# Keys kept unnormalised in the first layer of a four-layer network: their inverse norms reach the taps' sums through memory

## The chip, the cores and the metric

One core of a Trainium2 chip runs the whole network in one launch. The metric is the device time in microseconds (us). Three runs of the kernel before took 5038.33, 5038.93 and 5039.8 us; the median is 5038.93.

## What is computed

Four layers run one after the other over two images of 512 channels and 64 x 64 pixels, all in float32. Only the first layer matters here. It is an attention with 8 heads of 64 channels, in which each pixel attends to the 3 x 3 window around itself (nine "taps") and to 256 pooled tokens:

```python
q_norm = _l2norm(q)                                  # per pixel and head
q_scaled = (q_norm + query_embedding[None]) * softplus(temperature)[None]
k_l = _l2norm(k_l.reshape(B, N, nh, hd)).reshape(B, N, C)
...   # k_local, v_local: the 3 x 3 patches of keys and values, zeros outside the image
attn_local = jnp.einsum('bhnd,bhndk->bhnk', q_scaled, k_local)
attn_pool = jnp.einsum('bhnd,bhpd->bhnp', q_scaled, _l2norm(k_pool))
attn = softmax(concatenate([attn_local, attn_pool], -1), -1)
lt = jnp.einsum('bhnd,hdk->bhnk', q_norm, learnable_tokens) + learnable_bias[None] + a_local
x_local = jnp.einsum('bhnk,bhndk->bhnd', lt, v_local)
```

A score of a tap is a sum over the 64 channels of a head of query times key. The key's norm is one number for each pixel and head, so it may be multiplied into the key before the sum or into the sum after it.

## The kernel before

**Tiling.** Channels lie on the 128 partitions, so a tile holds two heads; there are four such chunks (`cc`). Pixels run along the free dimension. A unit is 1024 pixels (16 image rows) of one chunk: four units a chunk, 16 units an image, each in two halves `j` of 512 pixels. Keys and values of a chunk lie in SBUF as padded images `kx` and `vx` of 66 x 66 with zeros in the frame, so that a tap is a shifted view of them.

**Steps.** `Local.run` (L2046) is a software pipeline: in step `i` (from -4 to 16) several generators advance in turn, one round of all of them after the other, some ten rounds a step. In step `i`

- `projections` (L2349) projects keys of unit `i+4` and queries of unit `i+3` on TensorE (four matmuls of 128x512 for each half, by the helper at L134), and values. ScalarE reads each bank twice: once with the bias into `kraw` or `qn` (L2359), once squared into `sq` (L2361).
- `norms` (L2385) sums the squares that the step before left (L2395), and VectorE turns them (L2398), takes inverse roots by three Newton steps (L2401 to L2408) and turns them back into rows (L2410).
- `normed` (L2414) spreads a row over the 64 partitions of its head by a matmul with two rows of weights (L2422), and VectorE multiplies the raw keys into `kx` and the queries into `qn` (L2430): keys in one round, queries in the next. `learned` (L2438) then makes the learned tokens' term (L2445, L2448) and the scaled queries (L2450).
- `tap_products` (L2462) multiplies the scaled queries of unit `i+1` with the nine shifted views of `kx`, two taps in one instruction (L2473). The third of these is held until the last multiply of `normed` has been issued. `tap_sums` (L2490) sums the products over the channels of a head into one bank `tap` (L2500): row `32q + 2k + h` is tap `k` and head `h`, where `q` is 2 times the half plus `k % 2`. ScalarE takes Exp of that bank (L2508).
- `attend` (L2512) does unit `i`: scores against pooled tokens (L2525), Exp (L2529), values (L2535), sums (L2551, L2554), division, and stores the taps' weights to memory, `rows` (L2592).
- `weigh` (L2612) does unit `i-1`: ten weights (number 0 for the pooled part, 1 to 9 for taps) are fetched from memory, spread over 64 partitions each (L2610, two transfers a weight), copied to PSUM by ScalarE (L2626), multiplied by VectorE (L2634, L2631) and added by GpSimd (L2639). Three buffers take turns, so a fetch waits for the addition three weights before.

Before step 1 the pooled tokens are made (`pooled_tokens`, L2093) and their keys and values (`pooled_heads`, L2133), whose matmuls stand at L2151, L2160, L2177, L2211 and L2217. After the last unit the layer's output is projected.

**What sets the order.** PSUM gives five banks `mm` in a ring to everything but the queries' copy `qs` and the bank `tap`. From step 1 to step 11 (`steady`) TensorE keeps the order in which the program is written; the other engines, and all of them in the other steps, are put in order by a scheduler at build time. All transfers are issued by SyncE (SP), in order.

Of the kernel before, what the change touches and what calls it, by code (L numbers as in the profile page):

```python
# [9 lines left out]
F32 = mybir.dt.float32  # L10
I32 = mybir.dt.int32
AF = mybir.ActivationFunctionType
# [4 lines left out]
P = 128  # L17
# [1950 lines left out]
class Local:  # L1968
# [9 lines left out]
    def __init__(self, net, X, Y, sp_scale, d, wp, yp, pp, ppt, pps):  # L1978
# [3 lines left out]
        nc, new = self.nc, lambda shape, name: wp.tile(shape, F32, name=name)  # L1982

        self.yd = yp.tile([P, KC, N], F32, name="yd")
        self.wd = yp.tile([3, P, KC, C], F32, name="wd")
        self.rows = cycle([yp.tile([P // 2, self.UT], F32, name=f"rows{i}") for i in range(2)]).__next__

# [37 lines left out]
        self.raw = {"k": self.kraw, "q": self.qn}  # L2025
# [20 lines left out]
    def run(self):  # L2046


        self.nmean = self.net.stats[:, 0]
        xs = self.pooled_tokens()  # L2050
        heads = self.pooled_heads(xs)
        units = KC * self.UN
        unit = lambda u: u if 0 <= u < units else None
        self.pending = []
        for i in "qkv":
            self.fetch(i, 0)
        for i in range(-4, units + 1):
            k, q, ahead, u, before = (unit(i + n) for n in (4, 3, 1, 0, -1))
            self.steady = 1 <= i < units - 4
            streams, ended = [], []  # L2060
            stages = [self.norms(streams, ended)]
            if ahead is not None:
                stages.append(self.tap_products(ahead))
            if u is not None:
                stages.append(self.attend(u))
            if i == units:
                stages.append(self.output(KC - 2))
            if before is not None:
                stages.append(self.weigh(before))
# [23 lines left out]
    def pooled_tokens(self):  # L2093
# [13 lines left out]
        for blk in range(NB):  # L2107
# [14 lines left out]
            if 1 <= blk <= 3:  # L2122
# [5 lines left out]
                                  self.sq[i], self.vec[:, at:at + KC])  # L2128
                nc.sync.dma_start(self.wd[i], w3)
        self.frame(self.kx)  # L2130
        return xs

    def pooled_heads(self, xs):  # L2133
# [212 lines left out]
        self.net.project(ps, self.w[which], self.X, blk)  # L2346
        return ps

    def projections(self, uk, uq, uvs, streams):  # L2349

        nc = self.nc

        def project(u, which, j):
# [12 lines left out]
        last = KC * self.UN - 1  # L2366
        if last in uvs:
            uvs = []
        elif last - 1 in uvs:

            uvs = [last - 1, last]
        values = [(u, j) for u in uvs for j in range(2)]
        made, taken = ((4, 6, 7, 8), (0, 2)) if self.steady else ((6, 7, 8, 9), (0, 3, 6, 9))
        for step in range(10):
            if step in made:
                i = made.index(step)
                project((uk, uq)[i // 2], "kq"[i // 2], i % 2)
            if step in taken and values:
                u, j = values.pop(0)
                self.value(u, j)  # L2380
                if j and self.last(u):
                    self.fetch("v", u // self.UN + 1)
            yield

    def norms(self, streams, ended):  # L2385
# [22 lines left out]
            nc.vector.scalar_tensor_tensor(n if i == 2 else y, a, 1.5, y, ALU.add, ALU.mult)  # L2408
        rows = self.sq[1]
        nc.vector.transpose(rows, ps)  # L2410
        ended += [(s, rows[32 * s:32 * s + 2, :], *a) for s, a in enumerate(before)]
        yield

    def normed(self, ended):  # L2414

        nc = self.nc
        for _ in range(3 if self.steady else 5):
            yield
        for which in "kq":
            mine = [(e, self.bank()) for e in ended if e[2] == which]  # L2420
            for (s, rows, *_), ps in mine:
                nc.tensor.matmul(ps, self.cst[32 * s:32 * s + 2, C_ROW:C_ROW + P], rows, start=True,  # L2422
                                 stop=True)
            for (_, _, _, u, j, part, _), ps in mine:
                out = part
                if which == "k":
                    y = 1 + u % self.UN * self.UY + j * self.UY // 2
                    out = self.kx[:, y:y + self.UY // 2, 1:W + 1]
                    part, ps = (a.rearrange("p (y x) -> p y x", x=W) for a in (part, ps))
                self.multiplied = nc.vector.tensor_tensor(out, part, ps, ALU.mult).ins  # L2430
            yield
        if self.steady:
            yield
        if mine:
            self.learned(mine[-1][0][3])
        yield

    def learned(self, u):  # L2438

        nc, cc, qn = self.nc, u // self.UN, self.raw["q"]  # L2440
        ps = self.bank()
        for j in range(2):
            for g in range(2):
# [8 lines left out]

    def value(self, u, j):
        ps = self.projected("v", u % self.UN * 2 + j)
        y = 1 + u % self.UN * self.UY + j * self.UY // 2
        self.nc.scalar.activation(self.vx[:, y:y + self.UY // 2, 1:W + 1],
                                  ps.rearrange("p (y x) -> p y x", x=W), AF.Identity,
                                  bias=self.bias["v"][:, u // self.UN:][:, :1])

# [23 lines left out]
    def shifted(self, y, k, n):  # L2483
# [3 lines left out]
        part, rows, cols = a.ap  # L2487
        return bass.AP(a.tensor, a.offset + at(k), [part, [at(k + 1) - at(k), n], rows, cols])

    def tap_sums(self, u):  # L2490

        nc = self.nc
# [4 lines left out]
        for k in range(9):  # L2497
            for j in range(2):
# [337 lines left out]
```

## Time and profile before

| what | value |
|---|---|
| median of three runs | 5038.93 us |
| the profiled execution | 5044.18 us, its span 5042.3 us |
| granted TensorE clock, mean | 0.984 |
| TensorE busy (matmuls) | 4811.1 us, 95% of the span |
| VectorE busy | 3078.9 us, 61% |
| ScalarE busy | 1814.7 us, 36% |
| GpSimd busy | 1858.9 us, 37% |
| moved by DMA | 307.72 MB |

The page gives busy time of each engine, then groups of instructions by line of the kernel. PE is TensorE, PEld its loads of weights, DVE VectorE, ACT ScalarE, POOL GpSimd; SPq is SyncE's queue, in which a transfer counts for the time of its issue. A group such as L134 holds many calls of one helper. A matmul in float32 shows two records, and its end is modelled, so that the time from one group's start to the next group's start says more than the sum of durations. The timeline shows starting time, duration, engine, line, what is written and read, and in brackets how long the engine sat idle before and what released it. The two images show the layer twice, from about 30 us and from about 2540 us on; all times quoted are those of the first image.

### The profile page before, as it was taken

Reading aid. Unit: us, or ns where it says so; the run is one execution under the profiler, and the core shown is the slowest. Engines: PE = TensorE matmul, PEld = TensorE weight load, DVE = VectorE, ACT = ScalarE, POOL = GpSimd, SP = SyncE. Lnnn points to the kernel's source line nnn. Section 1 sums busy time; section 2 is a strip of 40 time slices with the busy share of each in tenths; the row PEclk is TensorE's granted clock in tenths of the full one; section 3 lists DMA queues with packets and bytes.
Section 4 is the critical chain, followed back from the end, with each engine's and each line's share of the span. In section 5 each row is a group of like instructions: output and inputs, shape, how many; then the busy total and the mean of one; then the engine's idle time right before and its main releaser. Section 6 shows DMA issues by size and latency. Waiting matters only on the chain. (4 is left out here: it accounts for less than half of the span.)

```text
span 5042.3 us, 48033 instructions
## 1 busy us (share of the span) xinstructions
PE 4811.1 (95%) x17027; PEld 1980.8 (39%) x17027; DVE 3078.9 (61%) x4020; ACT 1814.7 (36%) x3477; POOL 1858.9 (37%) x1218
## 2 busy tenths in 40 slices
PE   7999999999999999999999999999999999999998
PEld 3433332555334444433343333335543344444333
DVE  4267777754679633477733677777436795334776
ACT  1245555334323233322112555552443232333221
POOL 0036666501320145454500466664014101554554
PEclk9999999999999999999999999999999999999999
DMA  3035556600000000211120355565000000000111
GB/s 153 0 80 147 148 145 176 168 19 10 1 17 0 2 1 1 69 57 44 57 74 0 101 148 148 145 181 142 19 10 1 17 1 1 1 1 24 40 45 45
DMA packets 124172, 307.72 MB, mean 61 GB/s; under 512 B 20818, under 2 KB 33618, under 8 KB 122388
## 3 DMA queue, kind: packets, MB, share of 16 engines
q1 hardware_dynamic: 123924, 304.58, 20.9%
q8 instruction: 136, 2.23, 0.2%
q14 instruction: 112, 0.92, 0.1%
HBM read 256.01 MB, written 48.50 MB: 60 GB/s over the span
## 5 line engine op out<-in xcount | busy, mean ns | idle before, releaser
L134 PE MATMUL mm<-big,w 128*128 128x512 f32 x2496 | 1175.1, 614 | 30.1 <-DVE big L2430 11.7
L134 PEld LDWEIGHTS mm<-big,w 128*128 128x128 f32 x2496 | 455.3, 192 | 715.7 <-issue 553.0
L2639 POOL TENSOR_TENSOR late<-late,big 128x1024 f32<-128x1024 f32 x194 | 460.2, 2372 | 232.9 <-DVE big L2634 201.5
L2473 DVE TENSOR_TENSOR prods<-qs,big 128x1024 f32<-128x1024 f32 (+1 forms) x200 | 334.1, 1686 | 76.5 <-PE tap L2500 66.3
L1669 POOL TENSOR_TENSOR big<-big 128x512 f32<-128x512 f32 x224 | 278.0, 1273 | 219.0 <-ACT big L1660 219.0
L2634 DVE TENSOR_TENSOR big<-big,mm 128x512 f32<-128x512 f32 x388 | 254.7, 681 | 121.4 <-ACT mm L2626 120.6
L2626 ACT COPY mm<-big 128x512 f32<-128x512 f32 x432 | 248.1, 597 | 107.6 <-DMA big<-rows 59.0
L1660 ACT ACTIVATE big<-mm,ed 128x256 f32<-128x256 f32 x512 | 194.1, 490 | 233.0 <-DVE top L1656 200.3
L2544 POOL TENSOR_TENSOR late<-late 128x512 f32<-128x512 f32 x84 | 105.5, 1277 | 432.2 <-ACT late L2529 410.1
L2639 POOL TENSOR_TENSOR late<-late,tap 128x1024 f32<-128x1024 f32 x94 | 222.3, 2364 | 98.8 <-DVE tap L2634 79.9
L1472 POOL TENSOR_TENSOR wq<-prob 128x512 f32<-128x512 f32 x48 | 71.8, 1518 | 488.1 <-ACT prob L1469 476.7
L1656 DVE TENSOR_REDUCE top<-mm 128x1 f32<-128x512 f32 x256 | 159.0, 683 | 148.1 <-PE mm L1587 148.1
L1924 PE MATMUL mm<-k,w 128*128 128x512 f32 x512 | 236.6, 605 | 12.4 <-DVE k L1917 7.5
L134 PE MATMUL mm<-big,wq 128*128 128x512 f32 x512 | 236.7, 608 | 2.7 <-ACT off_t L1243 2.7
L1382 PE MATMUL acc<-big,diag 128*128 128x512 f32 x512 | 229.0, 605 | 9.8 <-ACT diag L1387 4.6
L1215 PE MATMUL mm<-big,wo 128*128 128x512 f32 x512 | 238.1, 611 | 0.0
L1634 PE MATMUL mm<-w,big 128*128 128x512 f32 x512 | 234.4, 601 | 0.0
L973 POOL TENSOR_TENSOR group_stats<-group_stats,cst 128x1 f32<-128x1 f32 (+1 forms) x20 | 20.2, 1027 | 564.6 <-DVE group_stats L972 508.2
L1914 DVE RECIPROCAL psD<-psD 128x512 f32<-128x512 f32 x64 | 215.1, 3362 | 1.9
L134 PE MATMUL mm<-big,big 128*128 128x512 f32 x464 | 201.7, 594 | 0.5 <-DVE b_sr L1011 0.5
L1469 ACT ACTIVATE prob<-mm 128x512 f32<-128x512 f32 x256 | 133.4, 602 | 171.6 <-PE mm L1466 171.3
L1556 POOL TENSOR_TENSOR sq<-k 128x512 f32<-128x512 f32 x128 | 133.1, 1042 | 155.2 <-ACT k L1554 139.1
(425 smaller groups left out, 8219.2 us busy)
## 6 DMA issues: line engine op xcount, KB each, us to landing
big<-rows SPq DMA_DIRECT2D x432, 256.0 KB, 4.2
tap<-rows SPq DMA_DIRECT2D x208, 256.0 KB, 4.1
yd<-late SPq DMA_DIRECT2D x32, 512.0 KB, 3.1
lost_all<-lost SPq DMA_DIRECT2D x128, 128.0 KB, 3.1
out<-big SPq DMA_DIRECT2D x64, 256.0 KB, 2.0
big<-in_W_kv SPq DMA_DIRECT2D x8, 1024.0 KB, 10.3
rows<-late SPq DMA_DIRECT2D x64, 128.0 KB, 3.6
big<-in_x SPq DMA_DIRECT2D x32, 256.0 KB, 3.6
```

The lines of the kernel that those rows point to most:

```text
L134: self.nc.tensor.matmul(ps, w[:, kc, :], X[:, kc, blk * TB:(blk + 1) * TB], start=(kc == 0), stop=(kc == KC - 1))
L1215: nc.tensor.matmul(ps, w[:, kc, oc * P:(oc + 1) * P], att[:, kc, :], start=(kc == 0), stop=(kc == KC - 1))
L1382: nc.tensor.matmul(accs[b], dg, src[:, b * TB:(b + 1) * TB], start=(j == 0), stop=(j == 6))
L1634: nc.tensor.matmul(ps, X[:, kc, lo:lo + P], wv[:, kc, :], start=(kc == 0), stop=(kc == KC - 1))
L1660: nc.scalar.activation(f[:, t, :], pS[h][i][:, t % 2, :], AF.Exp, bias=ed[:, t, 2 * cc + h:2 * cc + h + 1])
L1669: nc.gpsimd.tensor_tensor(a, a, part, ALU.add)
L1914: nc.vector.reciprocal(psD, psD)
L1924: nc.tensor.matmul(ps, self.wo[:, kc, oc * P:(oc + 1) * P], qs[:, kc, :], start=(kc == 0), stop=(kc == KC - 1))
L2473: self.nc.vector.tensor_tensor(self.pair(u, k)[:, :n].rearrange("p k (y x) -> p k y x", x=W), bcast(qs.rearrange("p (y x) -> p y x", x=W), ...
L2626: nc.scalar.copy(ps, part)
L2634: nc.vector.tensor_tensor(part.rearrange("p (y x) -> p y x", x=W), self.vx[:, y:y + self.UY // 2, dx:dx + W], ps.rearrange("p (y x) -> p y ...
L2639: nc.gpsimd.tensor_tensor(out, out, t, ALU.add)
```

## The change

- Keys are projected one step later, with the queries of the same unit (`i+3` for both). ScalarE writes them with their bias straight into `kx`, unnormalised (`rows_of` gives the rows of a unit there). `kraw` holds no keys any more, and `normed` treats queries only; it now does so in the round in which it treated keys, which is also the round of the first values of `attend`. `learned` stays in its round.
- The inverse norms of keys go from their row in SBUF to a new array in memory, `inverse`, of 24 rows (six for each chunk: two heads by three shifts of one pixel), with a margin of 65 numbers at both ends, which is filled once. One transfer for each half of a unit writes three shifted copies.
- `tap_inverses` reads them back for the unit of the taps: 12 transfers of 6 partitions by 512 numbers (four quarters of the partitions by three image rows) into half of `kraw`, laid out as the bank of the taps' sums is; for the last unit into a piece of the values' weights. Those rows of it that are never written are set to zero once.
- VectorE multiplies the bank of the taps' sums with it, ahead of Exp.

The changed program has 64 matmuls at the place of L2422 where there were 128, 128 of L2395 where there were 136, 64 new writes of `inverse`, 384 new reads and 32 new multiplies.

```diff
         self.yd = yp.tile([P, KC, N], F32, name="yd")
+        self.edge = W + 1
+        self.inverse = yp.tile([6 * KC, N + 2 * self.edge], F32, name="inverse")
...
-            k, q, ahead, u, before = (unit(i + n) for n in (4, 3, 1, 0, -1))
+            made, ahead, u, before = (unit(i + n) for n in (3, 1, 0, -1))
...
-            stages.append(self.projections(k, q, values, streams))
+            stages.append(self.projections(made, values, streams))
...
         self.frame(self.kx)
+        nc.gpsimd.memset(self.kraw[:, :TB], 0.0)
+        for at in (0, self.edge - 1 + N):
+            nc.sync.dma_start(self.inverse[:, at:at + self.edge + 1],
+                              self.cst[:6 * KC, :self.edge + 1])
...
-            part = self.raw[which][:, j * TB:(j + 1) * TB]
-            nc.scalar.activation(part, ps, AF.Identity, bias=b)
+            if which == "q":
+                part = self.qn[:, j * TB:(j + 1) * TB]
+                nc.scalar.activation(part, ps, AF.Identity, bias=b)
+            else:
+                part = None
+                nc.scalar.activation(self.rows_of(self.kx, u, j),
+                                     ps.rearrange("p (y x) -> p y x", x=W), AF.Identity, bias=b)
...
         nc.vector.transpose(rows, ps)
-        ended += [(s, rows[32 * s:32 * s + 2, :], *a) for s, a in enumerate(before)]
+        for s, (which, u, j, part, _) in enumerate(before):
+            row = rows[32 * s:32 * s + 2, :]
+            if which == "q":
+                ended.append((s, row, u, j, part))
+                continue
+            at = self.edge + 1 + u % self.UN * self.UT + j * TB
+            a = self.inverse[u // self.UN * 6:][:2, at:at + TB]
+            heads, cols = a.ap
+            nc.sync.dma_start(bass.AP(a.tensor, a.offset, [heads, [2 * heads[0] - 1, 3], cols]),
+                              bcast(row, 1, 3))
...
-        for which in "kq":
-            mine = [(e, self.bank()) for e in ended if e[2] == which]
-            for (s, rows, *_), ps in mine:
-                nc.tensor.matmul(ps, self.cst[32 * s:32 * s + 2, C_ROW:C_ROW + P], rows, start=True,
-                                 stop=True)
-            for (_, _, _, u, j, part, _), ps in mine:
-                out = part
-                if which == "k":
-                    y = 1 + u % self.UN * self.UY + j * self.UY // 2
-                    out = self.kx[:, y:y + self.UY // 2, 1:W + 1]
-                    part, ps = (a.rearrange("p (y x) -> p y x", x=W) for a in (part, ps))
-                self.multiplied = nc.vector.tensor_tensor(out, part, ps, ALU.mult).ins
-            yield
-        if self.steady:
+        mine = [(e, self.bank()) for e in ended]
+        for (s, rows, *_), ps in mine:
+            nc.tensor.matmul(ps, self.cst[32 * s:32 * s + 2, C_ROW:C_ROW + P], rows, start=True,
+                             stop=True)
+        for (*_, part), ps in mine:
+            self.multiplied = nc.vector.tensor_tensor(part, part, ps, ALU.mult).ins
+        for _ in range(3 if self.steady else 2):
             yield
...
+    def tap_inverses(self, u):
+        inverse = (self.kraw[:, :TB] if u < KC * self.UN - 1
+                   else self.w3[:, 2].rearrange("p k o -> p (k o)"))
+        for q in range(4):
+            for dy in range(3):
+                at = u % self.UN * self.UT + q // 2 * TB + dy * W + 1
+                self.nc.sync.dma_start(inverse[32 * q + 6 * dy:][:6, :],
+                                       self.inverse[u // self.UN * 6:][:6, at:at + TB])
+        return inverse
...
                                  start=(k < 2), stop=(k > 6))
+            if k == 3:
+                inverse = self.tap_inverses(u)
             if k % 2:
                 for _ in range(((2, 2, 3, 1) if self.steady else (2, 2, 2, 1))[k // 2]):
                     yield
+        nc.vector.tensor_tensor(ps, ps, inverse, ALU.mult)
         el = self.els()
         nc.scalar.activation(el, ps, AF.Exp)
```

More of the change, by code (lines that the diff above doesn't have):

```diff
@@ L2024, in __init__ @@
         self.bias = {i: new([P, KC], "b_" + i) for i in "qkv"}
-        self.raw = {"k": self.kraw, "q": self.qn}
         self.w, self.lt, self.el, self.out = {}, {}, {}, {}
@@ L2347, in projected, with rows_of, projections, project @@
         return ps
-    def projections(self, uk, uq, uvs, streams):
+    def rows_of(self, a, u, j):
+        y = 1 + u % self.UN * self.UY + j * self.UY // 2
+        return a[:, y:y + self.UY // 2, 1:W + 1]
+    def projections(self, u, uvs, streams):
         nc = self.nc
-        def project(u, which, j):
+        def project(which, j):
             if u is None:
@@ L2376, in projections @@
                 i = made.index(step)
-                project((uk, uq)[i // 2], "kq"[i // 2], i % 2)
+                project("kq"[i // 2], i % 2)
             if step in taken and values:
[L2379 to L2382, printed above, removed]
+                v, j = values.pop(0)
+                self.value(v, j)
+                if j and self.last(v):
+                    self.fetch("v", v // self.UN + 1)
             yield
@@ L2418, in normed @@
             yield
-        for which in "kq":
-            mine = [(e, self.bank()) for e in ended if e[2] == which]
-            for (s, rows, *_), ps in mine:
-                nc.tensor.matmul(ps, self.cst[32 * s:32 * s + 2, C_ROW:C_ROW + P], rows, start=True,
-                                 stop=True)
-            for (_, _, _, u, j, part, _), ps in mine:
-                out = part
-                if which == "k":
-                    y = 1 + u % self.UN * self.UY + j * self.UY // 2
-                    out = self.kx[:, y:y + self.UY // 2, 1:W + 1]
-                    part, ps = (a.rearrange("p (y x) -> p y x", x=W) for a in (part, ps))
-                self.multiplied = nc.vector.tensor_tensor(out, part, ps, ALU.mult).ins
-            yield
-        if self.steady:
+        mine = [(e, self.bank()) for e in ended]
[5 more added lines that the diff above has]
+        for _ in range(3 if self.steady else 2):
             yield
         if mine:
-            self.learned(mine[-1][0][3])
+            self.learned(mine[-1][0][2])
         yield
     def learned(self, u):
-        nc, cc, qn = self.nc, u // self.UN, self.raw["q"]
+        nc, cc, qn = self.nc, u // self.UN, self.qn
         ps = self.bank()
@@ L2454, in value @@
         ps = self.projected("v", u % self.UN * 2 + j)
-        y = 1 + u % self.UN * self.UY + j * self.UY // 2
-        self.nc.scalar.activation(self.vx[:, y:y + self.UY // 2, 1:W + 1],
+        self.nc.scalar.activation(self.rows_of(self.vx, u, j),
                                   ps.rearrange("p (y x) -> p y x", x=W), AF.Identity,
```

## The prediction, made before the change was run

> **What bounds the kernel now.** I read the page first, then busy time by stretches of one step, then the timeline of one step engine by engine, then single lines.
>
> ```profile
> PE 4811.1 (95%) x17027; PEld 1980.8 (39%) x17027; DVE 3078.9 (61%) x4020; ACT 1814.7 (36%) x3477; POOL 1858.9 (37%) x1218
> ```
>
> ```profile
> core 0: us, PE busy (x) PEld busy (x) DVE busy (x) ACT busy (x) POOL busy (x), PEclk, DMA share, GB/s
> 414.00:456.00 42.00, 41.30 (x152) 12.97 (x149) 31.56 (x48) 25.24 (x45) 25.65 (x14) 1.00 0.56 150
> 456.00:498.00 42.00, 41.30 (x152) 13.04 (x152) 31.26 (x46) 25.31 (x45) 25.63 (x14) 1.00 0.55 150
> ```
>
> A steady step of the first layer lasts 42.0 us (the products with norms of keys, L2422, come at 375.72 and again at 417.73). In it TensorE (PE) is busy for 41.3 us at full clock; VectorE (DVE) 31.5, ScalarE (ACT) 25, GpSimd (POOL) 26. So TensorE's own list of work sets the step, and what leaves this list shortens it, if nobody else becomes late. The timeline gives the price of the group that leaves:
>
> ```profile
> 377.90 3.70 PE L134 MATMUL mm<-big,w 128*128 128x512 f32 x8 [0.53 <-DVE big L2430]
> 381.53 1.13 PE L2422 MATMUL mm<-sq,cst 2*128 2x512 f32 x4
> 382.59 1.94 PE L2535 MATMUL mm<-late,vp 128*64 128x512 f32 x8
> ```
>
> From the start of L2422 to the start of the next group: 382.59 - 381.53 = 1.06 us for the two products of one unit (they share the array in time). At the layer's start it looks different:
>
> ```profile
> 167.20 6.16 PE L134 MATMUL mm<-big,w 128*128 128x512 f32 x8
> 173.19 1.89 PE L2177 MATMUL mm<-late,big 128*128 128x256 f32 x8
> ...
> 194.30 1.06 PE L2395 MATMUL mm<-sq,cst 128*32 128x512 f32 x8
> 195.30 0.44 PE L2198 MATMUL mm<-cst,late 128*128 128x128 f32 x2
> ...
> 204.86 2.08 PE L2422 MATMUL mm<-sq,cst 2*128 2x512 f32 x4 [2.45 <-DVE sq L2410]
> 206.87 18.91 PE L134 MATMUL mm<-big,w 128*128 128x512 f32 x40
> ```
>
> The first key's L2422 waits 2.45 us for its norms and then runs at half speed. The two projections of the first keys stand around L2177, under the pooled tokens' chain. Last, the DMA queue, which gets 14 more transfers in each step:
>
> ```profile
> L2610 SPq DMA_DIRECT2D big<-rows x432: 444/547/1468, 309.6 to 3494.9; - x144
> L2592 SPq DMA_DIRECT2D rows<-late x64: 460/588/1399, 306.6 to 3466.6; - x64
> ```
>
> ```profile
> 379.17 1.10 SPq L2610 DMA_DIRECT2D big<-rows  x2
> 383.97 1.08 SPq L2610 DMA_DIRECT2D tap<-rows  x2
> 388.36 3.51 SPq L2610 DMA_DIRECT2D big<-rows  x4
> ```
>
> SyncE (SP) needs 0.55 us for each issue (ns, least/median/most), about 24 issues or 13 us of a step's 42; it has room, but it works in order.
>
> **What the Trainium skill says.** "TensorE: Matmul & The Clock Gate", section "What's actually happening": an idle TensorE falls to half clock and must be busy for a while before it is fast again. The trace agrees: after the waits at 163 to 167 eight passes of L134 take 6.16 us, in the steady step 3.70. "DMA: Bandwidth & Descriptors", section "Two DMAs through the same engine are not ordered": a DMA that reads what another wrote must have its issuer wait for the first one's completion. The trace shows that wait in the kernel's own way through memory: L2610 waits for rows<-late 11 times in the steady steps, 31.7 us in total, 2.9 each. "Perfetto Trace Analysis", section "DMA Instruction — HWDGE (DVE, Sync)": the shown time of an issue is the descriptors' making, not the transfer. Here 0.55 us of issue stand against 4.1 us to landing.
>
> **The change part by part**, for one image (there are two), 16 units each.
>
> *Keys' products with norms go.* Units whose group lies in steps -2 to 12: 15 x 1.06 = 15.9 us off TensorE's list. VectorE loses two multiplies (L2430, 0.68 each) and gets one (128x512, out of and into PSUM; nearest row L2430, 0.68, and L2634, also 0.68): 0.68 less in each step, worth nothing alone, since VectorE isn't the bound. ScalarE writes the keys straight into the padded image: L2359 takes 0.69 us, and L2456, which writes values into just such rows, 0.69; nothing.
>
> *The first unit.* With the keys made one step later, step -3 has no norms at all: L2395 1.0 (194.30 to 195.30), the wait 2.45 and the slow L2422 2.0 (204.86 to 206.87): 5.5 us gone. What is late next is the pooled keys' chain, whose own waits (3.6 us for POOL L2205) stay.
>
> *The first keys' projections leave step -4 and come back in step 12.* They take 2 x 3.45 = 6.9 us at full clock. They covered VectorE's L2162 and the first L2164, which end at 169.2: without them L2177 waits 169.2 - 167.2 = 2.0 us. The half clock there then falls on L2177: the first projection really took 5.99 us, and I count only 3.45 of it as gone, so that the slow 2.5 stay; a longer idle time may cost up to as much again (bounds 0 and +2.5; I take 0). In step 12 the last keys' projections join the last queries': at most 2 x 3.63 = 7.3. That step has 2.8 us of TensorE waits in it today (0.24, 0.17, 1.09, 0.87, 0.46) and some 2.9 us lost to the half clock (L2551 3.30 instead of 1.94, L2422 1.90, L2525 1.64, L2554 1.36); so between +2 and +7.3; I take +5.5.
>
> *The new transfers.* The order of the built program shows where they stand on SP: the two writes of inverses around the fetch of tap 5 and before that of tap 6, the 12 reads together after tap 6's fetch, ahead of tap 7's. The rows of norms are ready at about 372.5 (L2410 ends at 414.5, one step of 42.0 before). Tap 6's fetch goes out at 379.17 because it waits for POOL; by then the writes, issued before 376, have landed (3.6 us, as rows<-late), so the first read waits for nothing. 12 reads x 0.55 = 6.6 us: 380.3 to 386.9. Tap 7's fetch is thus late by 2.9 us (383.97 before), and lands at 391.0 instead of 388.1. Who waits for that? ScalarE's copy of tap 7 (L2626). Before, its first half stood ahead of the key's second projection, at 388.72; in the changed order both halves stand after that projection's two reads and the learned sums, which end at about 393 - 1.06 + 0.9 = 392.9. Slack 1.9 us: hidden. The reads land by 390; the multiply that wants them comes after the last sums of taps, at 401.2 - 1.06: 10 us of cover.
>
> *The new multiply's wait.* VectorE waits for the last L2500, and behind it stands the next unit's second pair of products, which waits for the same L2500 today (L2473, 1.1 us at 402.31). It adds 0.68 us there; Exp follows 0.7 later, and the next sums of taps come only 6 us after. Nothing.
>
> *The queries a round earlier.* In the new order two large products (2.28 us each) stand together on VectorE, so tap 4's bank comes free 2.3 us later, at 383.7; the sums (L2551, 385.45 - 1.06 = 384.4) need it. Slack 0.7 us: small. ScalarE forms the scaled queries before the last exponentials, which end 1.7 us later, at 380.2; the values' products want them at 381.5. Small too. For both I charge 0.2 us in each of 16 steps, 3.2 us; the bounds are 0 and 0.5 (8).
>
> Sum: -15.9 - 5.5 - 6.9 + 2.0 + 5.5 + 3.2 = -17.6 us for an image, **-35 us** for both. Best ends: -15.9 - 5.5 - 6.9 + 2 + 2 = -24.3, so -49; worst: +2.5 for the clock, +7.3, +8: -8.5, so -17. The profiled execution took 5044.18 us (span 5042.3), 0.1% over the median 5038.93; I take the difference from the trace and set it on the median: **5004 us**, 4990 to 5022.
>
> **Rivals.**
> - *Slower: SP's burst starves the taps.* Place: tap 7's fetch behind the 12 reads. If a read of 6 partitions costs 1.0 us to issue (L2610's longest is 1.47, L2592's 1.40), the burst lasts 12 us, to 392.3; the tap lands at 396.4, ScalarE stands 3.5 us in order, PSUM banks stay taken and TensorE stands too: 22 steady steps x 3.5 = 77 - 35 = +42: **5081 us**. It decides from 0.71 us an issue (1.9 / 12 + 0.55), and eats the whole gain at about 0.84. Against: medians of 0.55 and 0.59, much larger transfers among them. For: short DMAs with few partitions are hardly in this trace.
> - *Nothing gained: banks and order.* The five PSUM banks turn over once a us; if the two slacks of 0.7 and 1.3 us fail together, TensorE waits 1 us in each of 32 steps instead of running L2422: about -35 + 32 = -3: **5036 us**. For: "L134 <-DVE big L2430" waits 0.53 us there already. Against: VectorE has 0.68 us less work in just that step.
> - That the change doesn't do what it says: the built program has 64 such products where there were 128, so no.
>
> **How the numbers follow.** Forecast 0.64, within 4990 to 5022. Nothing gained 0.14 (5029 to 5049). Slower 0.22, from 5049 on, half of it under 5085. To leave out no more than 2 in 10 the range must take in the second case and the low end of the third: 4988 to 5052. 0.2% of 5039 is 10 us, about what a measurement of this kernel can tell from no change: faster 0.65, same 0.13, slower 0.22.
>
> **What would show it.** Right: the steady step at about 41.1 us instead of 42.0; 64 matmul pairs fewer; SP's reads at 0.5 to 0.6 us; no wait of ScalarE's tap copies for DMA over 2 us; a wait of 2 us ahead of the pooled keys' products. Wrong: a step of 42 us or more with TensorE waiting for VectorE's tap products or ScalarE for DMA; a wait of the new multiply for DMA; a step 12 longer by more than 7 us.

## The result, and the profile after

| | before | after |
|---|---|---|
| median | 5039.80 us (5038.33 to 5040.87, 5 runs) | 5018.60 us (5011.38 to 5022.50, 5 runs) |
| profiled execution | 5044.18 us, span 5042.3 | 5015.88 us, span 5014.0 |

The ratio is 0.9956, 95% interval [0.9945, 0.9967]: 21 us faster. The forecast was 35 us faster; the time lies inside the range, 15 us above the forecast. The two profiled executions differ by 28.3 us, because the one of before lies 4.4 us above its median and the one of after 2.7 below.

Lines of the original file have moved: L2395 is now L2410 (sums of squares), L2422 is L2445 (products with norms, queries only), L2430 is L2448, L2500 is L2527 (sums of taps), L2508 is L2538 (Exp), L2610 is L2640 (fetches of weights), L2626 is L2656, L2634 is L2664. New are L2434 (writes of inverses), L2513 (reads) and L2536 (the multiply).

The page's first part, and then the busy time of a steady step, cut from one group of sums of squares to the next:

```profile
PE 4771.4 (95%) x16883; PEld 1971.8 (39%) x16883; DVE 3074.1 (61%) x3958; ACT 1816.8 (36%) x3477; POOL 1859.1 (37%) x1220
```

```profile
core 0: us, PE busy (x) PEld busy (x) DVE busy (x) ACT busy (x) POOL busy (x), PEclk, DMA share, GB/s
388.40:429.90 41.50, 40.80 (x149) 12.87 (x148) 32.44 (x48) 25.45 (x45) 26.25 (x13) 1.00 0.57 151
```

144 records of matmuls are gone from PE, and the steady step lasts 41.5 us. The step before was 42.5, not the 42.0 that the prediction states. Its sums of squares start 42.54 us apart:

```profile
364.34 1.07 PE L2395 MATMUL mm<-sq,cst 128*32 128x512 f32 x8
...
406.88 1.07 PE L2395 MATMUL mm<-sq,cst 128*32 128x512 f32 x8
```

(The 375.72 from which the prediction measured lies inside a group of L2422 that had begun at 375.19.) The timeline of TensorE shows the one product that is left and the layer's new start:

```profile
168.51 8.72 PE L2182 MATMUL mm<-late,big 128*128 128x256 f32 x32 [1.88 <-issue]
...
194.45 19.69 PE L134 MATMUL mm<-big,w 128*128 128x512 f32 x40 [0.18 <-DVE kp L2224]
214.06 1.06 PE L2410 MATMUL mm<-sq,cst 128*32 128x512 f32 x8
215.06 3.70 PE L134 MATMUL mm<-big,w 128*128 128x512 f32 x8
219.89 1.13 PE L2445 MATMUL mm<-sq,cst 2*128 2x512 f32 x4 [1.13 <-DVE sq L2425]
...
399.27 1.13 PE L2445 MATMUL mm<-sq,cst 2*128 2x512 f32 x4
400.33 1.13 PE L2555 MATMUL mm<-big,kp 64*128 64x512 f32 x4
```

Ahead of L2182 TensorE now waits 1.88 us (2.0 were forecast); no sums of squares are made at 194.30 any more, and those of step -2 come at 214.06 instead of 225.72; and from L2445 to its successor it is still 1.06 us, now for the queries alone. SyncE's queue around the reads in one steady step (start, time of issue, number of transfers), and all waits of ScalarE's copies of tap weights for DMA between 330 and 700 us (us in total, times, longest):

```profile
440.02 1.08 SPq L2640 DMA_DIRECT2D tap<-rows  x2
441.78 0.24 SPq L2434 DMA_DIRECT2D inverse<-sq  x1
444.75 1.08 SPq L2640 DMA_DIRECT2D big<-rows  x2
445.93 5.15 SPq L2513 DMA_DIRECT2D big<-inverse  x12
451.56 1.09 SPq L2640 DMA_DIRECT2D big<-rows  x2
```

```profile
ACT mm L2656 <- DMA big<-rows: 0.9, 1, 0.9
```

Twelve reads take 5.15 us, 0.43 each with the gaps, where 0.55 were assumed; ScalarE waits for a fetch once, 0.9 us, where it waited 11 times and 7.7 us before. So much went well. The layer's end didn't. These are the last sums of taps of a unit, the transfers and the multiply in step 12 (781 to 798) and in step 13, as TensorE, SyncE and VectorE saw them:

```profile
781.66 1.04 PE L2527 MATMUL tap<-prods,cst 128*32 128x512 f32 x2
...
798.07 1.92 PE L2527 MATMUL tap<-prods,cst 128*32 128x512 f32 x2 [4.23 <-ACT late L2538]
...
831.98 1.05 PE L2527 MATMUL tap<-prods,cst 128*32 128x512 f32 x2
...
848.75 5.33 PE L2527 MATMUL tap<-prods,cst 128*32 128x512 f32 x18 [8.23 <-ACT late L2538]
```

```profile
788.34 4.72 SPq L2513 DMA_DIRECT2D big<-inverse  x12
...
829.84 0.27 SPq L2434 DMA_DIRECT2D inverse<-sq  x1
833.39 1.08 SPq L2640 DMA_DIRECT2D big<-rows  x2
834.57 5.15 SPq L2513 DMA_DIRECT2D big<-inverse  x12
```

```profile
796.69 0.69 DVE L2536 TENSOR_TENSOR tap<-tap,big 128x512 f32<-128x512 f32 x1
...
841.57 0.72 DVE L2609 STREAM_TRANSPOSE mm<-mm 128x512 f32<-128x512 f32 x1
...
844.36 2.37 DVE L2616 TENSOR_TENSOR late<-late 128x512 f32<-128x512 f32 x1
846.77 0.69 DVE L2617 TENSOR_TENSOR late<-late 128x512 f32<-128x512 f32 x1
847.38 0.69 DVE L2536 TENSOR_TENSOR tap<-tap,big 128x512 f32<-128x512 f32 x1
```

In step 13 the last sums of the unit are made by 833.0; the second write of inverses goes out at 829.84, the last read by 839.7; and VectorE takes the multiply at 847.38, behind the whole division (L2609 to L2617). There is one bank `tap`, so the next unit's sums wait 8.23 us for Exp. In step 12 the sums are made by 782.7, the last read goes out by 793.1, the multiply follows at 796.69, behind the division too, and the wait is 4.23 us. The list of what the multiply waited for, over the whole trace, has one entry:

```profile
L2536 DVE TENSOR_TENSOR tap<-tap,big x30: 667/700/700, 269.2 to 3335.7; 128x512 f32<-128x512 f32 x30
...
  PE tap L2527: 28.8, 24
```

Waits for the sums are all that it has: no wait for a transfer is recorded. The reads hold the multiply all the same. In a run below (ScalarE's queue, step 12 steady) it began 1.6 us after the issue of the last read, released by the reads. With this landing time it could have begun, by an estimate, at 794.7 in step 12 and at 841.4 in step 13. So 12.0 and 8.3 us of the time from sums to multiply are the reads' lateness, and 2.0 and 6.0 us are the place behind the division, in the order that the scheduler gave VectorE. TensorE has other work until 793.8 and 840.5; of its two waits, 12.5 us, some 8 are therefore the order's, by the same estimate.

Where the time went, image 1, from the starts of sums of squares (L2395 before, L2410 after) and of the first matmuls of L1466, which lie behind the layer's output:

| stretch | forecast | measured |
|---|---|---|
| up to the sums of step -2 | -5.5 - 6.9 + 2.0 = -10.4 | 225.72 to 214.06: -11.6 |
| to step 1 (three steps) | 3 x (-1.06 + 0.2) = -2.6 | 321.80 to 305.46: -16.3 in all, -4.7 here |
| steps 1 to 10 | 10 x (-0.86) = -8.6 | 747.21 to 720.31: -26.9, -10.6 here |
| step 11 | -0.9 | 790.73 to 764.07: -26.7, +0.2 here |
| step 12 | +5.5 - 0.9 = +4.6 | 833.96 to 815.12: -18.8, +7.8 here |
| from step 13 on | +0.2 | 1227.95 to 1213.54: -14.4, +4.4 here |
| sum | -17.6 | -14.4 |

Image 2 gives -16.7 more, so the two images' first layers are 31.1 us shorter in the traces (last L1466 at 3961.1 and 3930.0; under 1 us of that lies ahead of and between the layers), against 35 forecast. What follows the second one differs from trace to trace: it took 1078 to 1087 us in the traces of this study, though nothing in it was changed.

### The profile page after: what moved, and what is told of

Its sections match the earlier page's. It is cut to its first block, busy times and chain, and to the rows that moved or that the text cites. A ratio compares the mean times of both kernels' runs of the same rounds, so it can differ in the third digit from the quotient of the medians.

```text
span 5014.0 us, 48290 instructions
## 1 busy us (share of the span) xinstructions
PE 4771.4 (95%) x16883; PEld 1971.8 (39%) x16883; DVE 3074.1 (61%) x3958; ACT 1816.8 (36%) x3477; POOL 1859.1 (37%) x1220
## 5 line engine op out<-in xcount | busy, mean ns | idle before, releaser
L134 PE MATMUL mm<-big,w 128*128 128x512 f32 x2496 | 1164.9, 610 | 16.3 <-DVE big L2448 11.5
L2664 DVE TENSOR_TENSOR big<-big,mm 128x512 f32<-128x512 f32 x388 | 253.1, 681 | 114.9 <-ACT mm L2656 107.0
L2656 ACT COPY mm<-big 128x512 f32<-128x512 f32 x432 | 245.8, 597 | 60.4 <-DMA big<-rows 25.1
L2527 PE MATMUL tap<-prods,cst 128*32 128x512 f32 x1152 | 189.6, 620 | 29.2 <-ACT late L2538 26.5
```

What stands on the lines that cost most here:

```text
L134: self.nc.tensor.matmul(ps, w[:, kc, :], X[:, kc, blk * TB:(blk + 1) * TB], start=(kc == 0), stop=(kc == KC - 1))
L2656: nc.scalar.copy(ps, part)
L2664: nc.vector.tensor_tensor(part.rearrange("p (y x) -> p y x", x=W), self.vx[:, y:y + self.UY // 2, dx:dx + W], ps.rearrange("p (y x) -> p y ...
```

## The experiments

**Theory.** The gain is the 1.06 us of each unit and the start; it is partly lost in steps 12 and 13, where the inverses reach the multiply too late. **Rivals.** The transfers cost something in every step (SyncE's burst); the new order of the queries does the work, not the missing matmuls; the multiply itself, or VectorE's order, is what costs.

### Nothing but the matmuls removed

No writes, no reads, no multiply. The keys' norms are left out of the scores altogether.

```diff
-            if k == 3:
-                inverse = self.tap_inverses(u)
...
-        nc.vector.tensor_tensor(ps, ps, inverse, ALU.mult)
...
-            nc.sync.dma_start(bass.AP(a.tensor, a.offset, ...), bcast(row, 1, 3))
```

> Leaves out the keys' norms: no writes and reads of inverses, no multiply of the taps' sums. Theory (the new multiply holds the one bank of the taps' sums in steps 12 and 13, where TensorE waits 4.2 and 8.2 us for Exp in each image): step 12 falls from 51.0 to about 46 us and step 13 by about 8, so some 12 us an image, 4994 us in all. Rival (step 12 is long because the keys' projections moved into it): step 12 stays at 50 us or more, 5012 us. The steady step stays at 41.5 us in both; if the memory path costs something there too, it falls below 41.3.

Measured: 4989.62 us (4984.45 to 4991.58), ratio 0.9895 [0.9878, 0.9911]. The steady step is 41.5, exactly as in the changed kernel; steps 11 and 12 last 42.5 and 44.0 instead of 43.8 and 51.0, and no sums of taps wait for Exp:

```profile
761.89 1.07 PE L2410 MATMUL mm<-sq,cst 128*32 128x512 f32 x8
...
805.93 1.07 PE L2410 MATMUL mm<-sq,cst 128*32 128x512 f32 x8
```

So step 12 fell by more than the theory said, and step 13 didn't follow it: from step 13 on image 1 is only 1.2 us shorter than in the changed kernel, although the wait of 8.2 us is gone. TensorE waits for VectorE there instead (7.1 us between 805 and 900). What the transfers and the multiply cost, 29 us in medians and 21 in the traces of the two layers (last L1466 at 3909.2 instead of 3930.0), lies outside the steady steps.

### The multiply without the transfers

It multiplies with numbers that lie in SBUF already. The writes and reads, and so the keys' norms, are left out here too.

```diff
-        nc.vector.tensor_tensor(ps, ps, inverse, ALU.mult)
+        nc.vector.tensor_tensor(ps, ps, self.kraw[:, :TB], ALU.mult)
```

> Leaves out the keys' norms, but keeps the multiply: it reads a tile that is there all the time, and no inverses are written or read. If the reads' late landing makes the multiply late, this is as fast as the kernel without the whole memory path, about 4995 us, and the waits for Exp in steps 12 and 13 go. If VectorE's order does it (the multiply stands behind the division and four products), the waits stay at 4 and 8 us and the time at 5016 us.

Measured: 4999.50 us (4995.45 to 5002.20), ratio 0.9915 [0.9898, 0.9931]. Step 12 lasts 45.3, the stretch from step 13 on is 4.5 us shorter than in the changed kernel, and the waits for Exp in these steps are gone. The multiply alone is what separates this run from the one before: 10 us in medians, 4.3 in the traces (last L1466 at 3913.5 and 3909.2). VectorE and TensorE in its step 12 (the multiply is L2532 there, the sums L2525):

```profile
784.78 0.69 DVE L2532 TENSOR_TENSOR tap<-tap,big 128x512 f32<-128x512 f32 x1
...
789.62 0.72 DVE L2605 STREAM_TRANSPOSE mm<-mm 128x512 f32<-128x512 f32 x1
```

```profile
780.72 1.05 PE L2525 MATMUL tap<-prods,cst 128*32 128x512 f32 x2
```

Without transfers the multiply stands close behind the sums and ahead of the division. So it is neither the division as such nor VectorE's load that keeps the multiply back, but the transfers. Whether through their own lateness or through the place that the scheduler gives the multiply on their account, this run doesn't tell. In this trace image 1 is 24.4 us shorter than before (1227.95 to 1203.51), 10.0 more than in the changed kernel.

### Step 12 in the steady order

```diff
-            self.steady = 1 <= i < units - 4
+            self.steady = 1 <= i < units - 3
```

> Step 12 follows the steady steps' rounds and TensorE's written order. Theory: with keys and queries both in it, step 12 holds the same work as a steady step, so it takes 41.5 to 42.5 us instead of 51.0 and the wait of 4.2 us for Exp goes: -9 us an image, about 5000 us; the wait in step 13 stays. Rival (transfers for the end of the layer make step 12 long): 48 us or more, 5014 us.

Measured: 4994.77 us (4992.22 to 4999.79), ratio 0.9912 [0.9895, 0.9928]; 24 us below the changed kernel and the fastest of those that leave nothing out. Step 11 now lasts 41.5 and step 12 43.8, together 9.6 us less; the reads of step 12 are issued by 782.6 and the multiply, at 798.53, waits for the sums again. The wait of step 12 shrinks from 4.23 to 0.37; that of step 13 stays:

```profile
799.92 1.90 PE L2527 MATMUL tap<-prods,cst 128*32 128x512 f32 x10 [0.37 <-ACT late L2538]
...
838.60 5.33 PE L2527 MATMUL tap<-prods,cst 128*32 128x512 f32 x18 [8.15 <-ACT late L2538]
```

The two layers then end within 1.4 us of the run with nothing but the matmuls removed (last L1466 at 3910.6 and 3909.2), with transfers, multiply and the wait of step 13 in them. Whether the kernel before would also gain from one more steady step was not run.

### Steps 12 and 13 in the steady order

```diff
-            self.steady = 1 <= i < units - 4
+            self.steady = 1 <= i < units - 2
...
+        if len(values) > 2:
+            taken = (0, 2, 4, 6)
```

> Steps 12 and 13 both follow the steady steps' rounds and TensorE's written order. With step 12 alone steady the median was 4994.8 us, and the wait of 8.2 us for Exp at the end of step 13 was left. Theory (this wait comes from the late reads of inverses and the multiply put behind the division): in the steady order both are in time, the wait goes, and 6 to 8 us an image are gained: 4980 to 4984 us. Rival (step 13, without projections, has too little TensorE work to hide anything and becomes bound by VectorE or the taps' chain): 4992 us or more.

Measured: 4999.13 us (4993.19 to 5003.25), ratio 0.992 [0.9906, 0.9933]. The wait of 8.15 goes, and others take its place at the end of step 13 and in step 14:

```profile
835.13 2.68 PE L2529 MATMUL tap<-prods,cst 128*32 128x512 f32 x12 [1.77 <-ACT late L2540]
...
844.86 3.31 PE L2529 MATMUL tap<-prods,cst 128*32 128x512 f32 x12 [1.27 <-DVE prods L2491]
...
854.05 3.88 PE L2567 MATMUL mm<-late,vp 128*64 128x512 f32 x8 [4.81 <-DVE late L2663]
```

So the wait of 8 us in step 13 isn't worth 8 us: with it gone, VectorE's tap products (L2491) and its multiply of the pooled part (L2663) are late next, as the rival had it.

### Reads two rounds earlier in the program

```diff
-            if k == 3:
+            if k == (3 if self.steady else 1):
```

> Outside the steady steps the inverses are read two rounds earlier, nothing else. Theory (in steps 12 and 13 the writes and reads of inverses stand on SyncE behind taps' fetches that wait for GpSimd, so that the multiply, and with it the one bank of the taps' sums, is late): TensorE's waits for Exp of 4.2 and 8.2 us shrink to under 3 in sum, 8 to 10 us an image, 5000 us. Rival (VectorE's order alone, with the division first, makes it late): waits stay, 5016 us.

Measured: 5022.28 us (5015.84 to 5027.42), ratio 0.9962 [0.995, 0.9974]: no different from the changed kernel. SyncE issues the reads at 789.75 and 835.29 (788.34 and 834.57 in the changed kernel), still behind the writes and the fetches. The edit moved a line, and not the transfer; it tells nothing of the question.

### Writes and reads from ScalarE's queue

Outside the steady steps only.

```diff
-            nc.sync.dma_start(bass.AP(a.tensor, a.offset, ...), bcast(row, 1, 3))
+            (nc.sync if self.steady else nc.scalar).dma_start(..., bcast(row, 1, 3))
...
-                self.nc.sync.dma_start(inverse[32 * q + 6 * dy:][:6, :], ...)
+                (self.nc.sync if self.steady else self.nc.scalar).dma_start(...)
```

> The changed kernel with the writes and reads of the inverses issued by ScalarE in the steps that are not steady, so that they no longer stand behind tap fetches that wait for GpSimd on SyncE. Theory (the transfers come late there because of SyncE's order): the waits of the tap sums for Exp, 4.2 us in step 12 and 8.2 us in step 13, fall below 2 us, and up to 9.5 us are won for each image (what leaving the transfers out won): 5000 to 5006 us. A price: ScalarE stands some 3 us for the landing of the writes before its first read, which may take back half: up to 5012. Rival (the multiply comes late because VectorE has the division ahead of it): both waits stay, 5016 to 5021.

Measured: 5039.05 us (5036.88 to 5043.14), ratio 1.0 [0.9991, 1.0008]. Neither theory expected that. Counted from the step's sums of squares, the reads of steps 12 and 13 begin 4 us earlier than on SyncE (after 20.1 and 15.2 us; 24.3 and 19.5 there), but the last of them is out only after 28.4 and 27.3 us (29.0 and 24.6 there), and the multiply follows after 29.8 and 29.7 (32.6 and 32.3 there). It stands ahead of the division now; here the reads, and ScalarE that they hold, are what keeps it late. No waits for Exp are listed, but only because TensorE waits for others (4.5 and 5.8 us for products of L2664): ScalarE itself stands:

```profile
786.34 8.32 ACTq L2513 DMA_DIRECT2D big<-inverse  x12
794.70 0.59 ACT L2656 COPY mm<-tap 128x512 f32<-128x512 f32 x1 [9.57 <-DMA big<-inverse]
...
834.52 11.78 ACTq L2513 DMA_DIRECT2D big<-inverse  x11
846.34 0.59 ACT L2567 COPY late<-mm 128x512 f32<-128x512 f32 x1 [11.34 <-DMA big<-inverse]
```

The 12 reads hold ScalarE for 8 and 12 us, and VectorE and TensorE wait for its copies. A single issue takes 0.31 us here; the reads go out in groups with gaps of up to 3.7 us between them, whose cause the trace doesn't show. I had priced the landing of the writes (3 us), and neither the issues nor the gaps. SyncE, for which the same reads take 5.15 us, has no computing to hold up. The same two queues with step 12 steady:

> The changed kernel with step 12 in the steady order (4994.8 us by itself) and the writes and reads of the other steps issued by ScalarE. If the theory holds, the wait of 8.2 us for Exp that step 13 still has falls below 3 us, and some 4 us are won for each image: 4985 to 4990 us. If it doesn't hold, or ScalarE's own wait takes it back: 4993 to 4999.

Measured: 5017.52 us (5014.09 to 5019.34), ratio 0.9955 [0.9938, 0.9972], 23 us above the kernel with step 12 steady alone. The wait for Exp in step 13 is gone, as the theory said, but the loss is larger than even the rival had it: the reads hold ScalarE for 8.8 us. In step 13 of this trace the multiply stands ahead of the division and is released by the reads: they go out by 833.4, and it begins at 835.03, after 0.29 us of waiting for them.

### Only the writes from ScalarE's queue

Step 12 is here as in the changed kernel again, not in the steady order.

> As the kernel before it in this call, but only the writes of the inverses go to ScalarE; the reads stay on SyncE. If the writes are what comes late, the reads follow earlier too and most is won: 5002 to 5008 us. If it is the reads, behind the tap fetches, that come late, the waits of 4.2 and 8.2 us stay: 5016 to 5021.

Measured: 5007.41 us (5004.45 to 5016.19, 4 runs), ratio 0.9935 [0.9918, 0.9951]. The median is 11 us below the changed kernel, but the trace, which is that of the slowest of the four runs, shows both waits nearly as they were:

```profile
799.59 3.15 PE L2527 MATMUL tap<-prods,cst 128*32 128x512 f32 x16 [3.59 <-ACT late L2538]
...
849.25 5.33 PE L2527 MATMUL tap<-prods,cst 128*32 128x512 f32 x18 [8.43 <-ACT late L2538]
```

ScalarE issues the writes at 779.91, 782.67, 824.84 and 829.06, in order among its copies; SyncE did it at 777.15, 783.50, 826.43 and 829.84. So they went out hardly earlier, the reads end at 793.6 and 840.4 as before, and the run doesn't tell writes from reads. Where the median's 11 us come from, the trace doesn't show.

### Twice the reads in the steady steps

```diff
                 inverse = self.tap_inverses(u)
+                if self.steady:
+                    inverse = self.tap_inverses(u)
```

> The changed kernel with every read of the inverses issued twice in the 22 steady steps, so that the burst on SyncE is 24 reads. A read's issue was 0.43 us in the changed kernel, so 24 take 10.3 us instead of 5.15. The prediction gave the burst 8.5 us (6.6 plus a slack of 1.9) before tap 7 comes too late for ScalarE. If that working holds, each steady step gets up to 1.8 us longer: 43.3 at most, and the total lies between 5019 and 5058 us; I take 5040, with ScalarE's copies waiting for DMA in the steady steps. If SyncE's order has no bearing there (more slack than I worked out), the step stays at 41.5 and the total at 5019.

Measured: 5026.63 us (5022.97 to 5033.26), ratio 0.9973 [0.9965, 0.9982]: 8 us above the changed kernel, so in the interval, and 13 below the value I took. The burst, and ScalarE's waits for DMA between 330 and 700 us:

```profile
447.70 9.12 SPq L2513 DMA_DIRECT2D big<-inverse  x24
```

```profile
ACT mm L2658 <- DMA big<-rows: 28.7, 24, 2.2
...
ACT mm L2658 <- DMA tap<-rows: 15.7, 12, 2.2
```

Of the steady steps of image 1 most keep 41.5 us; three last 42.0, 43.2 and 42.4. The mechanism of the prediction's slower rival exists: with a burst of 9.1 us ScalarE begins to wait for fetches, 44.4 us in 370 where it was 0.9. The limit that the prediction worked out for the burst (6.6 + 1.9 = 8.5 us) fits that. But a microsecond of ScalarE's waiting is worth far less than one of the step, which the rival had taken as equal: the three steps are 3.2 us longer in sum.

### The queries one round later

As before the change, relative to the values' step.

```diff
-        for _ in range(3 if self.steady else 5):
+        for _ in range(4 if self.steady else 6):
...
-        for _ in range(3 if self.steady else 2):
+        for _ in range(2 if self.steady else 1):
```

> Puts the queries' products with norms one round later, where they were before the change. Theory: that move is worth nothing, since TensorE's list is the same: steady step 41.5 us, 5018 us, within 5. Rival: the earlier round is what keeps the scaled queries in time: steady step over 42 us and 5035 us or more.

Measured: 5085.46 us (5076.23 to 5096.86), ratio 1.0082 [1.0065, 1.0099]: within the rival's bounds, but slower than the kernel before too, which wasn't expected. The steady steps last 43.8 to 47.8. With this edit the third pair of tap products is released by a multiply of the step before, so the hold no longer holds. The next run tests that; in it the pair waits for the transpose that ends the norms:

```diff
-        nc.vector.transpose(rows, ps)
+        self.multiplied = nc.vector.transpose(rows, ps).ins
...
-            self.multiplied = nc.vector.tensor_tensor(part, part, ps, ALU.mult).ins
+            nc.vector.tensor_tensor(part, part, ps, ALU.mult)
```

> The queries' products with norms one round later again, but the third pair of tap products is held until the end of the norms' chain on VectorE instead of until the queries' multiply. The later round with the old hold took 5085 us. Theory A (that kernel was slow because the hold pointed at the multiply of the step before and so let a product of 2.3 us go ahead of the norms' chain): steady step 41.5 to 42 us, 5015 to 5030 us. Theory B (the round itself: the group on TensorE stands behind the keys' first projection, so that the queries are multiplied, scaled and learned late and banks stay taken): steady step 44 us or more, 5065 us or more.

Measured: 5026.76 us (5019.92 to 5041.39), ratio 0.9973 [0.9966, 0.9979]; steps of 42.3 to 44.5. TensorE's waits for the exponentials of the pooled scores between 330 and 700 us, first without the hold, then with it:

```profile
PE mm L134 <- ACT late L2559: 25.7, 16, 4.1
```

```profile
PE mm L134 <- ACT late L2559: 14.5, 17, 1.9
```

In the changed kernel that line reads 1.6 us. The time is that of theory A, the steps are a little longer than it said. So the earlier round is no price that was paid, but a part of the gain: some 8 us of medians, with the reserve that the two kernels hold the pair by different instructions.

### Without the hold

```diff
-            held = (self.net.tc.issue_after(self.multiplied) if self.steady and k == 4
-                    else nullcontext())
+            held = nullcontext()
```

> The changed kernel without the hold of the third pair of tap products. If the hold is what the queries' later round lost (theory A), the steady step is 44 us or more here as well and the time 5060 us or more. If the round itself matters (theory B), the step stays within 42 us and the time within 5030 us.

Measured: 5052.50 us (5048.13 to 5057.06), ratio 1.0024 [1.0015, 1.0033], 34 us above the changed kernel and between the two theories. Both hold in part: the hold is worth 34 us with the earlier round and 59 with the later one, the round 8 us with a hold and 33 without. Every step of the steady part now waits 1.5 us for the queries' multiply (0.5 in the changed kernel), and they last 42.4 or 44.1 us, the last 47.8. TensorE in two steps that follow each other:

```profile
491.57 3.70 PE L134 MATMUL mm<-big,w 128*128 128x512 f32 x8 [1.49 <-DVE big L2448]
...
534.01 5.23 PE L134 MATMUL mm<-big,w 128*128 128x512 f32 x8 [1.49 <-DVE big L2448]
```

The same wait costs 1.5 us in one step and 3.0 in the next, in which eight passes take 5.23 us instead of 3.70. The granted clock is 1.00 in the first of these steps and 0.96 in the second.

## Why the prediction was right, and where its sizes were off

- *Keys' products, 1.06 us a unit: right.* The steady step fell from 42.54 to 41.48. The price read from start to start of groups (1.06 for two matmuls whose records say 1.13) was the step's to the hundredth; TensorE was the bound and stayed it. That the step is 42.0 was a misreading, which no term of the sum used (it only put the rows of norms half a microsecond late).
- *First unit and first projections, -10.4: right, -11.6.* The wait ahead of L2182 was 1.88 us for 2.0 forecast. The three steps that follow gave 2.1 more than the sum had.
- *0.2 us a step for the queries' round: wrong sign.* In the steady steps it costs nothing (-1.06 a step against -0.86), and the runs with the queries one round later are slower, by 8 us if the hold is kept.
- *The last keys in step 12, +5.5: too much for what it priced.* Without transfers step 12 lasts 45.3, against 43.2 before; with the unit's 1.06 that also leaves it, the projections cost 3.1 us, near the lower bound (1.9 where the multiply is left out too).
- *"The new multiply's wait: nothing": this step failed,* in steps 12 and 13. The prediction worked out the steady step, where it holds, and charged the same nothing outside. In the steady step the last sums of taps end 36.9 us after the step's sums of squares, and the reads are out after 21.2: that is the cover. In step 12 the sums end after 18.6 us already, and the reads are out only after 29.0. The second write stands there behind a fetch that waits for GpSimd (783.50), the reads follow at 788 to 793, and the scheduler puts the multiply behind the division. That costs 10.0 us in image 1 and 6.5 in image 2 (last L1466 3930.0 against 3913.5, less image 1's 10.0), and 19 us in medians, all against the run that keeps the multiply and leaves out the transfers. It hit the very condition named as wrong: step 12 is 7.8 us longer than before. The other condition, a wait of the multiply for DMA, never came true in the changed kernel: the multiply stood behind other work for longer than the reads took to land.
- *SyncE's transfers hidden: right* in the steady steps. Issues took 0.43 us, the copies' waits for DMA fell from 7.7 to 0.9 us, and twice the reads cost only 8 us. The slower rival's threshold fits, its price doesn't: it made every microsecond of ScalarE's wait one of the step.
- *Nothing gained:* the wait it named (0.53 for L2430) is still 0.52 and didn't grow.

The Trainium skill's section "What's actually happening" in "TensorE: Matmul & The Clock Gate" says that the window over which TensorE's activity is watched runs freely, and that the point of transition depends on where in it the work lands. The run without the hold fits that: equal waits of 1.49 us, and only one of the two shown is followed by slow passes. The section puts the fall of the clock after an idle window of about 3.4 us; here a wait of 1.49, the longest of its step, was enough in some steps, and the measurement decides.

The forecast gain was 14 us larger than the measured one: 4 are in the layer, 3 in what follows it, and 7 in how the profiled executions stand to their medians. In the layer the missed 16.5 us of steps 12 and 13 are set against terms that were too cautious. That the layers' sum came within 4 us of the forecast is to that extent luck.

Not settled: why the scheduler put the multiply behind the division in steps 12 and 13. That it would stand ahead of it, if the scheduler's estimate of a transfer were another, wasn't tried. The shares of the reads and of the order in its lateness rest on a landing time that was seen on ScalarE's queue, not on SyncE's. Nor is it known what the kernel with the writes on ScalarE's queue won, or what the kernel before would win with the queries one round earlier.

## What to carry to other kernels

Read the price of a removed matmul from start to start of its neighbours in the stage that TensorE bounds; here it arrived in full. Work out the cover of a new transfer for the first and last steps of a pipeline too, where the order is another, and look in the built order at what stands ahead of its consumer: a late transfer need not show as a wait in the trace, if its consumer has been put behind other work. A transfer moved to a busy engine's queue costs that engine the time of its issue, and here the gaps between issues too. A wait that is removed is worth only what the next one leaves: the 8 us of step 13 were worth 1.2 in one run and 4.5 in another.

## What the runs showed of the hardware

- Twelve reads of 6 partitions by 512 numbers took 5.15 us of SyncE in a row (0.43 each; the issue alone 0.293 in the median), 24 of them 9.12; broadcasts to 64 partitions 0.55 each. On ScalarE's queue 11 and 12 of the same reads took 11.78 and 8.32 us, gaps in between included, at 0.31 us for one issue in the median.
- On ScalarE's queue, with step 12 steady, reads of 12 KB released the multiply 1.6 us after the last had been issued.
- A wait of TensorE of 1.49 us was followed by eight passes of 5.23 us in one step and by 3.70 in the step before; in the run with the queries later, one of 2.86 was followed by 6.75 and one of 2.83 by 3.70.
